# A hand-laid order for all engines in a recommendation kernel on one core: 11 steps a tile, each with a share of every kind of work

## The chip, the cores and the metric

The kernel runs on one core of a Trainium2 chip. A core has a matrix engine (PE, TensorE), a vector engine (DVE), a scalar engine (ACT), GpSimd (POOL), a sequencer for transfers (SP) and 16 DMA engines. Each engine works through its own instruction stream in the order in which the instructions stand there, and waits at an instruction until what it needs is there.

The metric is the time of one execution on the device in microseconds (us). For the kernel before it is 10250.98 us, the median of 3 runs (10248.7 to 10254.62). About 0.2% of that, 20 us, is what a measurement tells from no change.

## What is computed

16384 users, for each 32 token indices, three lists of 20 indices and four single indices. Rows of the word table (50000 x 300) are averaged over the 32 tokens; rows of three small tables (1000, 5000 and 10000 rows of 64) are averaged over the 20 indices; four tables (100, 50, 20 and 1000 rows of 64) give one row each. Each small table has a second, one column wide, whose rows are summed. The features, 748 wide, go through four layers.

```python
tok = word_emb[token_idx].mean(axis=1)
e1 = emb_mh1[mh1_idx].mean(axis=1)
...
o1 = emb_oh1[oh1_idx]
...
emb = jnp.concatenate([tok, e1, e2, e3, o1, o2, o3, o4], axis=1)
wide = (wide_mh1[mh1_idx].sum(axis=(1, 2)) + ... + wide_oh4[oh4_idx][:, 0])[:, None]
h = jax.nn.relu(emb @ W1 + b1)      # 748 -> 1024
h = jax.nn.relu(h @ W2 + b2)        # 1024 -> 512
h = jax.nn.relu(h @ W3 + b3)        # 512 -> 256
return jax.nn.sigmoid(h @ Wd + bd + wide)
```

## The kernel before

The 16384 users are 32 blocks of 512, and a block is four **tiles** of 128 users (one user to a partition).

**Small tables by matmul.** At the start the seven small tables are loaded and laid out in SBUF as 138 slices of 128 rows, each value split into three bf16 terms (`terms`, lines 132 to 155). A lookup with its sum is then a matmul: for each user a matrix of counts, 128 rows by 138 slices, says how often a table row is named. That matrix is made on the chip. `lookup_keys` (lines 200 to 231) turns the indices of a block into row and slice numbers. For eight pairs of users at a time DVE makes one-hot rows (`row1`) and one-hot slices (`slice1`) with a compare (L244), eight pieces a tile in two buffers. PE multiplies them (L255), two matmuls of half the partitions for each pair, 128 a tile, into a PSUM tile `pc` that holds three pairs and has two buffers. ACT writes each `pc` into `cnt` as fp8 (L263), 22 evictions a tile. `small_sums` then runs over the 138 slices, one matmul each with its weights in `cnt` and its data in `terms` (L281), into `pg`, two tables at a time, and DVE adds the three terms of each (L286), four reductions a tile.

**Word table by gathers.** `tokens` (lines 178 to 198) works in eight groups of four tokens. For each group POOL issues four indirect DMAs (L184), each of which fetches one row of 300 floats for each of 128 users, into `tok_rows`, which has three buffers. DVE folds the four to two (L192) and to one (L197) and adds that to `g` (L198); the first group writes `g` itself (L195).

**Layers.** `mlp` runs once a block: PE transposes the features in fp32 (L336), DVE scales them into `x` (L337), then come the layers (L321), 176 products of 128 x 128 by 128 x 512 in fp32, each of which PE runs as several passes, with ACT's relu behind each group of products (L328). Two PSUM buffers `ph` are shared by the transposes, the layers and the output row (L346, L348, sigmoid L352).

**What sets the order.** The program is written tile after tile: one-hots, counts, sums, tokens, wide sums of a tile, and the layers after four tiles. Before, a scheduler sorts each engine's instructions by their place in the program and by what is ready in its model, and so lets the counts of one tile and the sums of another stand between each other. POOL's gathers stay in program order. SP loads the indices.

Of the kernel before, what the change touches and what calls it, by code (L numbers as in the profile page):

```python
# [8 lines left out]
F32 = mybir.dt.float32  # L9
# [17 lines left out]
ONEHOT = 8  # L27
# [14 lines left out]
def kernel(  # L42
# [42 lines left out]
    gp = ctx.enter_context(tc.tile_pool(name="g", bufs=NSUB))  # L85
# [92 lines left out]
    def tokens(g, it):  # L178

        for q in range(N_TOK // TOK_GROUP):  # L180
            rows = tokp.tile([P, TOK_GROUP * TOK_D], F32, name="tok_rows")
            for t in range(TOK_GROUP):
                j = q * TOK_GROUP + t
                nc.gpsimd.indirect_dma_start(  # L184
                    out=rows[:, t * TOK_D : (t + 1) * TOK_D],
                    out_offset=None,
                    in_=word,
                    in_offset=bass.IndirectOffsetOnAxis(ap=it[:, j : j + 1], axis=0),
                )
            n = TOK_GROUP * TOK_D // 2  # L190
            while n > TOK_D:
                nc.vector.tensor_add(rows[:, 0:n], rows[:, 0:n], rows[:, n : 2 * n])  # L192
                n //= 2
            if q == 0:
                nc.vector.tensor_add(g[:, 0:n], rows[:, 0:n], rows[:, n : 2 * n])  # L195
            else:
                nc.vector.tensor_add(rows[:, 0:n], rows[:, 0:n], rows[:, n : 2 * n])  # L197
                nc.vector.tensor_add(g[:, 0:n], g[:, 0:n], rows[:, 0:n])  # L198

    def lookup_keys(blk):  # L200
# [5 lines left out]
        ix = keyp.tile([P, pairs, 2, N_SMALL], I32, name="ix")  # L206
        for s in range(NSUB):
            b0 = blk * BLOCK + s * P
            nc.sync.dma_start(
                out=ix[(s % 2) * HALF : (s % 2 + 1) * HALF, s // 2],  # L210
                in_=idx[b0 : b0 + P, IDX_MH:IDX_COLS].rearrange("(f p) c -> p f c", p=HALF),
            )
        part = keyp.tile([P, 2, pairs, 2, N_SMALL], I32, name="part")
        nc.vector.tensor_single_scalar(part[:, 0], ix, P - 1, op=ALU.bitwise_and)
        nc.vector.tensor_single_scalar(part[:, 1], ix, 7, op=ALU.logical_shift_right)
        keys = keyp.tile([P, pairs, 2, 2 * N_SMALL], BF16, name="keys")
        for r in range(pairs):
            view = keys[:, r].rearrange("p w (f c) -> p w f c", f=2)
            nc.vector.tensor_copy(view[:, 0], part[:, 0, r])
            nc.vector.tensor_add(view[:, 1], part[:, 1, r], first)  # L220
# [12 lines left out]
    def counts(sc, s):  # L233

        cnt = cp.tile([P, 2, HALF, n_h], FP8, name="cnt", tag="counts")
        pc = None
        for b in range(HALF):
            if b % ONEHOT == 0:
                row1 = ohp.tile([P, ONEHOT, P], BF16, name="row1")
                slice1 = ohp.tile([P, ONEHOT, n_h], BF16, name="slice1")  # L240
                hot = (row1, slice1)
                for w, (one, n) in enumerate(((row1, P), (slice1, n_h))):
                    shape = [P, ONEHOT, n // 2, 2]
                    nc.vector.tensor_tensor(  # L244
                        one.rearrange("p i (n d) -> p i n d", d=2),
                        iota[:, 0:n].rearrange("p (n d) -> p n d", d=2).unsqueeze(1).to_broadcast(shape),
                        sc[:, s // 2, w, s % 2, b : b + ONEHOT, :].unsqueeze(2).to_broadcast(shape),
                        ALU.is_equal,
                    )
            k = b % PER_BANK  # L250
            if k == 0:
                pc = ps_c.tile([P, 2, 512], F32, name="pc")
            for f in range(2):
                rows = slice(f * HALF, (f + 1) * HALF)
                nc.tensor.matmul(  # L255
                    pc[:, f, k * n_h : (k + 1) * n_h],
                    hot[0][rows, b % ONEHOT, :],
                    hot[1][rows, b % ONEHOT, :],
                    start=True,
                    stop=True,  # L260
                )
            if k == PER_BANK - 1 or b == HALF - 1:
                nc.scalar.activation(  # L263
                    cnt[:, :, b - k : b + 1, :].rearrange("l f k h -> l f (k h)"),
                    pc[:, :, 0 : (k + 1) * n_h],
                    AF.Copy,
                    scale=0.5,
                    saturate=True,
                )
        return cnt  # L270

    def small_sums(g, cnt):

        by_slice = cnt.rearrange("l f p h -> l (f p) h")
        for i in range(0, len(SMALL), 2):
            pair = SMALL[i : i + 2]
            pg = ps_g.tile([P, 2, 3 * ROW], F32, name="pg")
            for j, f in enumerate(pair):
                h0, h1 = slices[f]
                for h in range(h0, h1):  # L280
                    nc.tensor.matmul(  # L281
                        pg[:, j, :], by_slice[:, :, h], terms[:, h, :], start=(h == h0), stop=(h == h1 - 1)
                    )
            at = TOK_D + i * ROW
# [6 lines left out]
            )  # L291

    def features(it, sc, s):

        g = gp.tile([P, G_COLS], F32, name="g")
        small_sums(g, counts(sc, s))
        tokens(g, it)
# [9 lines left out]
        return g, wide  # L307

    def chunk(g, k):
# [5 lines left out]
        return g[:, at : at + 2 * EMB]  # L315

    def layer(dst, weights, bias, src, kks, n_out):
        for m in range(n_out):
            ph = ps_h.tile([P, BLOCK], F32, name="ph", tag="ph")
            for k, kk in enumerate(kks):  # L320
# [6 lines left out]
                )  # L327
            nc.scalar.activation(dst[:, m, :], ph, AF.Relu, bias=bias[:, m : m + 1])  # L328

    def mlp(blk, gs):  # L330
        x = xp.tile([P, NK, BLOCK], F32, name="x", tag="even")
        for k in range(NK):
            kk = chunk_k[k]
            pt = ps_h.tile([P, BLOCK], F32, name="pt", tag="ph")
            for s, (g, _) in enumerate(gs):
                nc.tensor.transpose(pt[:kk, s * P : (s + 1) * P], chunk(g, k), ident)  # L336
            nc.vector.tensor_scalar(x[:kk, k, :], pt[:kk, :], scale[:kk, k : k + 1], None, ALU.mult)  # L337
        h1 = xp.tile([P, M1, BLOCK], F32, name="h1", tag="odd")
        layer(h1, w1_sb, b1_sb, x, chunk_k, M1)
        h2 = xp.tile([P, M2, BLOCK], F32, name="h2", tag="even")  # L340
        layer(h2, w2_sb, b2_sb, h1, [P] * M1, M2)
        h3 = xp.tile([P, M3, BLOCK], F32, name="h3", tag="odd")
        layer(h3, w3_sb, b3_sb, h2, [P] * M2, M3)
# [3 lines left out]
        for s, (_, wide) in enumerate(gs):  # L347
            nc.tensor.matmul(  # L348
                po[:, s * P : (s + 1) * P], wide, ident, start=False, stop=(s == NSUB - 1)
            )  # L350
# [4 lines left out]
        )  # L355

    for blk in range(B // BLOCK):
        it = idxp.tile([P, NSUB, N_TOK], I32, name="it")
        nc.sync.dma_start(
            out=it,  # L360
            in_=idx[blk * BLOCK : (blk + 1) * BLOCK, 0:N_TOK].rearrange("(s p) c -> p s c", p=P),
        )
        sc = lookup_keys(blk)
        mlp(blk, [features(it[:, s, :].bitcast(U32), sc, s) for s in range(NSUB)])


# [39 lines left out]
```

## Time and profile before

| | us |
|---|---|
| median of 3 runs | 10250.98 |
| the profiled execution's own time | 10252.28 |
| its span, first to last instruction | 10250.5 |
| length of one block (a 32nd of the steady part) | 317.5 |

The profile is one execution. Its page gives each engine's busy time and its share of the span, a strip of 40 equal slices, the DMA queues, the chain of work that ended last, and groups of instructions: line, engine, operation, what it writes and reads, the tile's shape, how often, then busy microseconds and the mean of one in nanoseconds, then the idle time just before them and what ended most of it. PE's weight loads are listed as PEld; they overlap its matmuls. "issue" stands for idle time for which the profile shows no cause. The mean clock granted to PE over the span was 0.709 of full speed. In the busy strip all slices but the first and the last few look alike, so a stretch of a few tiles from the middle can stand for the whole:

```profile
PE   3666666666566656666566665666656666666666
...
DVE  4333333333333343333333333333333333333332
ACT  3222222222222222222222222222222222222222
POOL 5334433334333343333433334333343333433332
PEclk7776667776677766777667776677766777667777
```

### The profile page before, as it was taken

What the parts mean: (1) busy time and instruction counts of PE and PEld (TensorE: products, weight loads), DVE (VectorE), ACT (ScalarE), POOL (GpSimd) and SP (SyncE); (2) the same over time, 40 slices, a digit from 0 to 9 for tenths busy, and PEclk for the clock granted to TensorE, in tenths of its full rate; (3) what the DMA queues carried; (4) which work ended last, traced back from release to release, by engine and by line L of the source; (5) the groups of instructions that cost most, each with busy time, mean ns of one, the idle gap of its engine ahead of it and who ended that gap; (6) DMA issues with size and microseconds to landing.
All of it is one profiled execution on the core that took longest, in us unless ns stands there. A gap on an engine that the chain in (4) does not pass through costs nothing.

```text
span 10250.5 us, 99707 instructions
## 1 busy us (share of the span) xinstructions
PE 6613.1 (65%) x40960; PEld 4044.7 (39%) x40960; DVE 3434.1 (34%) x6209; ACT 2584.4 (25%) x3385; POOL 4006.1 (39%) x4103
## 2 busy tenths in 40 slices
PE   3666666666566656666566665666656666666666
PEld 2443434444344433434334433434334344343444
DVE  4333333333333343333333333333333333333332
ACT  3222222222222222222222222222222222222222
POOL 5334433334333343333433334333343333433332
PEclk7776667776677766777667776677766777667777
DMA  4222222222222222222222222222222222222221
GB/s 118 60 58 68 68 65 58 60 63 72 61 59 59 63 76 60 59 57 63 78 60 59 59 59 78 59 59 59 58 78 59 62 59 59 74 62 62 59 58 44
DMA packets 242805, 652.31 MB, mean 64 GB/s; under 512 B 105631, under 2 KB 109471, under 8 KB 242347
## 3 DMA queue, kind: packets, MB, share of 16 engines
q0 software_dynamic: 196608, 629.41, 22.8%
q1 hardware_dynamic: 42738, 10.83, 0.5%
q8 instruction: 320, 5.24, 0.2%
q10 hardware_dynamic: 3001, 5.69, 0.2%
q14 instruction: 138, 1.13, 0.0%
HBM read 645.59 MB, written 0.07 MB: 63 GB/s over the span
## 4 chain that ended last, share of the span: by engine, by line
issue 59%; POOL 31%; PE 5%; DMA 1%; ACT 1%; DVE 1%; another core or an unknown queue 1%; POOLq 0%; SPq 0%; DVEq 0%; ACTq 0%
POOL tok_rows L184 31%; PE pg L281 2%; PE ph L321 2%; DMA tok_rows<-in_word_emb_dram,it 1%; ACT cnt L263 1%; PE pc L255 0%; DVE slice L244 0%; DMA raw<-in_mh_dram 0%; DVE tok_rows L192 0%; DVE row L244 0%; ACT h L328 0%; PE pt L336 0%; DVE g L286 0%; POOLq L184 0%
## 5 line engine op out<-in xcount | busy, mean ns | idle before, releaser
L184 POOL DMA_INDIRECT tok_rows<-in_word_emb_dram,it x4096 | 4005.2, 978 | 6120.9 <-DVE g L195 3741.5
L281 PE MATMUL pg<-terms,cnt 128*128 128x195 bf16 x17664 | 2323.1, 285 | 2037.1 <-issue 2000.2
L263 ACT ACTIVATE cnt<-pc 128x828 fp8e3<-128x828 f32 (+1 forms) x2816 | 2140.4, 850 | 4317.8 <-PE pc L255 4277.9
L281 PEld LDWEIGHTS <-cnt 128*128 128x128 fp8e3 x17664 | 1927.2, 147 | 2487.5 <-issue 2446.0
L255 PE MATMUL pc<-slice,row 64*128 64x138 bf16 x16384 | 1473.7, 304 | 1004.4 <-ACT cnt L263 695.4
L192 DVE TENSOR_TENSOR tok_rows<-tok_rows 128x600 f32<-128x600 f32 x1024 | 799.7, 781 | 2858.7 <-DMA tok_rows<-in_word_emb_dram,it 2845.8
L321 PE MATMUL ph<-x,w_sb 128*128 128x512 f32 (+1 forms) x3072 | 1462.2, 638 | 449.3 <-ACT h L328 435.2
L255 PEld LDWEIGHTS <-row 64*128 64x128 bf16 x16384 | 869.2, 123 | 1510.0 <-issue 1334.3
L328 ACT ACTIVATE h<-ph,b_sb 128x512 f32<-128x512 f32 x448 | 305.8, 687 | 3292.3 <-PE ph L321 2228.3
L321 PEld LDWEIGHTS ph<-x,w_sb 128*128 128x128 f32 (+1 forms) x3072 | 622.5, 205 | 1270.0 <-issue 771.7
L321 PE MATMUL ph<-h,w_sb 128*128 128x512 f32 x2560 | 1103.9, 592 | 0.0
L286 DVE TENSOR_REDUCE g<-pg 128x130 f32<-128x390 f32 (+1 forms) x512 | 247.8, 510 | 1960.7 <-PE pg L281 1949.5
L244 DVE TENSOR_TENSOR row<-iota,sc 128x1024 bf16<-128x1024 bf16 x1024 | 705.2, 689 | 197.4 <-PE pc L255 178.2
L244 DVE TENSOR_TENSOR slice<-iota,sc 128x1104 bf16<-128x1104 bf16 x1024 | 743.6, 726 | 0.0
L321 PEld LDWEIGHTS ph<-h,w_sb 128*128 128x128 f32 x2560 | 486.4, 190 | 612.3 <-issue 612.3
L227 DVE COPY sc<-pk 128x1024 bf16<-128x1024 bf16 x32 | 39.2, 1225 | 1643.4 <-PE pk L224 1643.4
L198 DVE TENSOR_TENSOR g<-g,tok_rows 128x300 f32<-128x300 f32 x896 | 420.2, 469 | 23.9
L197 DVE TENSOR_TENSOR tok_rows<-tok_rows 128x300 f32<-128x300 f32 x896 | 420.8, 473 | 17.5
L336 PE MATMUL pt<-ident,g 128*128 128x128 f32 (+1 forms) x768 | 221.1, 370 | 102.1 <-DVE sc L227 40.9
L336 PEld LDWEIGHTS pt<-ident,g 128*128 128x128 f32 (+1 forms) x768 | 108.1, 167 | 198.4 <-issue 94.9
L337 DVE TENSOR_SCALAR x<-pt,scale 128x512 f32<-128x512 f32 (+1 forms) x192 | 140.1, 746 | 3.4 <-PE pt L336 0.6
L346 PE MATMUL po<-h,wd_sb 128*1 128x512 f32 x128 | 60.1, 591 | 0.0
(35 smaller groups left out, 391.0 us busy)
## 6 DMA issues: line engine op xcount, KB each, us to landing
tok_rows<-in_word_emb_dram,it POOLq DMA_INDIRECT x4096
ix<-in_idx_dram SPq DMA_DIRECT2D x128, 32.0 KB
w_sb<-in_W_dram ACTq DMA_DIRECT2D x6, 512.0 KB
w_sb<-in_W_dram ACTq DMA_DIRECT2D x1, 2048.0 KB
it<-in_idx_dram SPq DMA_DIRECT2D x32, 64.0 KB
out_dram<-y SPq DMA_DIRECT2D x32, 2.0 KB
raw<-in_mh_dram SPq DMA_DIRECT2D x1, 422.5 KB
w_sb<-in_W_dram ACTq DMA_DIRECT2D x1, 256.0 KB
```

Source lines behind the costliest of these rows:

```text
L184: nc.gpsimd.indirect_dma_start(out=rows[:, t * TOK_D : (t + 1) * TOK_D], out_offset=None, in_=word, in_offset=bass.IndirectOffsetOnAxis(ap ...
L192: nc.vector.tensor_add(rows[:, 0:n], rows[:, 0:n], rows[:, n : 2 * n])
L197: nc.vector.tensor_add(rows[:, 0:n], rows[:, 0:n], rows[:, n : 2 * n])
L198: nc.vector.tensor_add(g[:, 0:n], g[:, 0:n], rows[:, 0:n])
L244: nc.vector.tensor_tensor(one.rearrange("p i (n d) -> p i n d", d=2), iota[:, 0:n].rearrange("p (n d) -> p n d", d=2).unsqueeze(1).to_broa ...
L255: nc.tensor.matmul(pc[:, f, k * n_h : (k + 1) * n_h], hot[0][rows, b % ONEHOT, :], hot[1][rows, b % ONEHOT, :], start=True, stop=True,)
L263: nc.scalar.activation(cnt[:, :, b - k : b + 1, :].rearrange("l f k h -> l f (k h)"), pc[:, :, 0 : (k + 1) * n_h], AF.Copy, scale=0.5, sat ...
L281: nc.tensor.matmul(pg[:, j, :], by_slice[:, :, h], terms[:, h, :], start=(h == h0), stop=(h == h1 - 1))
L286: nc.vector.tensor_reduce(g[:, at : at + n * ROW].rearrange("p (f d) -> p f d", f=n), pg[:, 0:n, :].rearrange("p f (c d) -> p f d c", c=3) ...
L321: nc.tensor.matmul(ph, weights[:kk, k, m * P : (m + 1) * P], src[:kk, k, :], start=(k == 0), stop=(k == len(kks) - 1),)
L328: nc.scalar.activation(dst[:, m, :], ph, AF.Relu, bias=bias[:, m : m + 1])
L336: nc.tensor.transpose(pt[:kk, s * P : (s + 1) * P], chunk(g, k), ident)
```

## The change

The scheduler is switched off (`manual_schedule`), and the program itself writes every engine's order. A tile now has 11 steps. The pieces of work are generators, and a small class, `Paced`, lets each advance by its share at every step. A step holds:

- the counts of six pairs of users of this tile, 12 matmuls and two evictions (the last step four pairs), and the one-hots for the step after it;
- an eleventh of the token groups of this tile: in eight of the eleven steps one group, its gathers and its adds;
- an eleventh of the sums of the **preceding** tile, 13 to 15 matmuls; after the fourth table's pair the count of work takes in a lull of 12;
- a 44th of the layers of the **preceding block**.

At the end of a tile come the wide sums of the preceding one; at the end of a block its six groups of transposes and the copies to `x`, not spread over steps. After the last tile one more round does the last sums, and then the last block's layers run alone. `g` has five buffers instead of four; `tok_rows` keeps three, `onehot` and `counts` two. The index loads of a block are issued in the second tile of the block before it. The order of the tables within the sums is (0, 2, 6, 4) instead of (0, 2, 4, 6). The number of operations of each other kind stays, but the one-hots come in 11 pieces a tile instead of eight.

```diff
-ONEHOT = 8
+ONEHOT = 6
+STEPS = -(-HALF // ONEHOT)
+LULL = 12
...
-    gp = ctx.enter_context(tc.tile_pool(name="g", bufs=NSUB))
+    gp = ctx.enter_context(tc.tile_pool(name="g", bufs=NSUB + 1))
...
     def small_sums(g, cnt):
-        for i in range(0, len(SMALL), 2):
+        for i in (0, 2, 6, 4):
...
+                    if h < h1 - 1:
+                        yield 1
...
+            yield n if i != 6 else n + LULL
...
+    class Paced:
+        def __init__(self, gen, size, n):
+            self.gen, self.size, self.n = gen, size, n
+            self.done = self.part = 0
+        def go(self):
+            self.part += 1
+            while self.done * self.n < self.size * self.part:
+                work = next(self.gen, None)
+                if work is None:
+                    return
+                self.done += work
...
+    mlp_size = NK * M1 + M1 * M2 + M2 * M3 + M3
+    ctx.enter_context(tc.manual_schedule())
...
+    for t in range(tiles + 1):
+        s = t % NSUB
+        sums = None
+        if before:
+            sums = Paced(small_sums(*before), n_h + LULL, STEPS)
+        if t < tiles:
...
+            toks = Paced(tokens(g, it[:, s, :].bitcast(U32)), N_TOK // TOK_GROUP, STEPS)
+        for i in range(STEPS):
+            if t < tiles:
+                hot_now = hot
...
+                if i < STEPS - 1:
+                    hot = one_hots(sc, s, i + 1)
...
+                counts(cnt, hot_now, i)
+                toks.go()
+            if sums:
+                sums.go()
+            if layers:
+                layers.go()
+        if before:
+            sums.finish()
+            gs.append(before[0])
+            wides.append(wide_term(before[0]))
+        before = (g, cnt) if t < tiles else None
+        if len(gs) == NSUB:
+            if layers:
+                layers.finish()
+            layers = Paced(mlp(t // NSUB - 1, transposed(gs), wides), mlp_size, NSUB * STEPS)
+            gs, wides = [], []
+    layers.finish()
```

The lines have new numbers: gathers L184 are now L186, the adds L192, L197 and L198 are L194, L199 and L200, the one-hots L244 are L255, counts L255 are L273, evictions L263 are L280, sums L281 are L298, their reductions L286 are L305, layers L321 are L348 and relus L328 are L357.

The instructions of DVE in the middle of a tile, before. `x2` after a row means two in a row; `tok_rows` are the gathered word rows, `g` the features, `pg` the sums of the small tables.

```order
L286 TENSOR_REDUCE g<-pg 128x130
L195 TENSOR_TENSOR g<-tok_rows 128x300
L198 TENSOR_TENSOR g<-g,tok_rows 128x300 x2
L192 TENSOR_TENSOR tok_rows<-tok_rows 128x600
L197 TENSOR_TENSOR tok_rows<-tok_rows 128x300
L198 TENSOR_TENSOR g<-g,tok_rows 128x300
```

The first add into `g` (L195) stands behind the reduction of the first sums (L286), and the adds of the other groups follow it one after another with nothing between them. The same engine after the change, from a like place:

```order
L255 TENSOR_TENSOR row_6163<-iota,sc 128x768
L255 TENSOR_TENSOR slice_6164<-iota,sc 128x828
L194 TENSOR_TENSOR tok_rows<-tok_rows 128x600
L199 TENSOR_TENSOR tok_rows<-tok_rows 128x300
L200 TENSOR_TENSOR g<-g,tok_rows 128x300
L305 TENSOR_REDUCE g<-pg 128x130
L255 TENSOR_TENSOR row_6208<-iota,sc 128x768
L255 TENSOR_TENSOR slice_6209<-iota,sc 128x828
```

Each group's adds now stand between the one-hots of two steps, with a reduction among them now and then.

ACT before, over one block: the evictions of the counts of four tiles (`cnt` from `pc`), and the relus of the layers (`h` from `ph`) together at its end.

```order
L263 ACTIVATE cnt<-pc 128x2x414 x21
L263 ACTIVATE cnt<-pc 128x2x138
L328 ACTIVATE h_7513<-ph,b_sb 128x512 x8
L328 ACTIVATE h_7578<-ph,b_sb 128x512 x4
L328 ACTIVATE h_7619<-ph,b_sb 128x512 x2
L352 ACT_TABLE_LOAD
L352 ACTIVATE y<-po,bd_sb 1x512
```

And after the change:

```order
L357 ACTIVATE h_30037<-ph,b_sb 128x512
L280 ACTIVATE cnt<-pc 128x2x414 x8
L357 ACTIVATE h_30037<-ph,b_sb 128x512
L280 ACTIVATE cnt<-pc 128x2x414 x3
L280 ACTIVATE cnt<-pc 128x2x138
L280 ACTIVATE cnt<-pc 128x2x414 x4
L357 ACTIVATE h_30037<-ph,b_sb 128x512
```

The relus no longer stand together: a few evictions lie between any two of them.

More of the change, by code (lines that the diff above doesn't have):

```diff
@@ L231, in lookup_keys @@
         return sc
[L233 to L248, printed above, removed]
-                    )
[L250 to L270, printed above, removed]
@@ L306, in features @@
         nc.vector.tensor_add(wide, wide, g[:, G_COLS - 1 : G_COLS])
-        return g, wide
+        return wide
     def chunk(g, k):
@@ L355, in mlp, with finish @@
         )
[L357 to L364, printed above, removed]
+        yield M3
+    class Paced:
[9 more added lines that the diff above has]
+                self.done += work
+        def finish(self):
+            for _ in self.gen:
+                pass
```

114 lines of the change are left out of this document (88 added, 26 removed).

## The prediction, made before the changed kernel ran

> **What bounds the kernel now.** I read the page first: no engine is busy for two thirds of the span, and the chain that ended last is mostly "issue".
>
> ```profile
> span 10250.5 us, 99707 instructions
> PE 6613.1 (65%) x40960; PEld 4044.7 (39%) x40960; DVE 3434.1 (34%) x6209; ACT 2584.4 (25%) x3385; POOL 4006.1 (39%) x4103
> issue 59%; POOL 31%; PE 5%; DMA 1%; ACT 1%; DVE 1%; another core or an unknown queue 1%; POOLq 0%; SPq 0%; DVEq 0%; ACTq 0%
> ...
> L184 POOL DMA_INDIRECT tok_rows<-in_word_emb_dram,it x4096 | 4005.2, 978 | 6120.9 <-DVE g L195 3741.5
> L281 PE MATMUL pg<-terms,cnt 128*128 128x195 bf16 x17664 | 2323.1, 285 | 2037.1 <-issue 2000.2
> L263 ACT ACTIVATE cnt<-pc 128x828 fp8e3<-128x828 f32 (+1 forms) x2816 | 2140.4, 850 | 4317.8 <-PE pc L255 4277.9
> L255 PE MATMUL pc<-slice,row 64*128 64x138 bf16 x16384 | 1473.7, 304 | 1004.4 <-ACT cnt L263 695.4
> ```
>
> The sums (L281) stood idle 2037 us, 2000 of them for nothing that the profile shows. The timeline of one tile shows how that looks:
>
> ```profile
> 5028.10 0.32 PE L281 MATMUL pg<-terms,cnt 128*128 128x195 bf16 x1 [1.08 <-issue]
> 5030.23 0.32 PE L281 MATMUL pg<-terms,cnt 128*128 128x195 bf16 x1 [1.81 <-issue]
> ...
> 5037.22 0.95 POOL L184 DMA_INDIRECT tok_rows<-in_word_emb_dram,it  x1 [0.30 <-issue]
> 5038.48 0.95 POOL L184 DMA_INDIRECT tok_rows<-in_word_emb_dram,it  x1 [0.30 <-issue]
> ...
> 5043.56 1.30 PE L281 MATMUL pg<-terms,cnt 128*128 128x195 bf16 x7 [0.38 <-issue]
> ...
> 5065.64 14.21 PE L281 MATMUL pg<-terms,cnt 128*128 128x195 bf16 x137 [0.75 <-ACT cnt L263]
> ```
>
> With no gather running, 137 sums take 14.21 us. While gathers are issued every 1.26 us (5037.22 to 5038.48), sums come one at a time, some 2 us apart, until 5.1 us after the last gather began. Then they are dense at once. So I asked for the busy time of stretches cut at the gathers (columns: length, then busy us and instructions of PE, PEld, DVE, ACT, POOL; PE clock; DMA):
>
> ```profile
> 4886.89:4917.00 30.11, 11.62 (x98) 9.07 (x96) 6.74 (x12) 0.00 (x0) 22.86 (x24) 0.71 0.44 118
> 4928.81:4941.00 12.19, 7.78 (x80) 4.46 (x80) 8.12 (x14) 9.79 (x13) 8.75 (x8) 0.50 0.38 101
> ...
> 5084.62:5126.40 41.78, 32.33 (x70) 13.61 (x68) 11.47 (x20) 2.75 (x4) 30.73 (x32) 0.92 0.44 118
> ...
> 4941.00:4948.32 7.32, 4.84 (x38) 4.43 (x38) 4.84 (x9) 1.55 (x3) 0.00 (x1) 0.57 0.01 2
> ```
>
> A run of 24 gathers lets PE through 98 matmuls in 30 us, one of 32 lets through 70 in 42 us, but one of 8 beside the counts lets through 80 in 12 us. A burst passes something like a hundred matmuls and then almost none. ACT is caught too: in the run of 32 it did four instructions.
>
> **The bound per tile.** Two prices, each for one of the 128 tiles. Gathers: 32 at 1.26 us, 40.3 us. PE's own work, from its dense rows:
>
> ```profile
> 5143.17 34.50 PE L321 MATMUL ph<-h,w_sb 128*128 128x512 f32 x80
> 5177.60 1.88 PE L346 MATMUL po<-h,wd_sb 128*1 128x512 f32 x4
> 5179.31 1.04 PE L348 MATMUL po<-ident,wide 128*1 128x128 f32 x8
> ...
> 5183.37 0.87 PE L255 MATMUL pc<-slice,row 64*128 64x138 bf16 x12 [0.94 <-DVE slice L244]
> ...
> 5081.89 1.29 PE L336 MATMUL pt<-ident,g 128*128 128x128 f32 x8 [1.20 <-DVE wide L306]
> ```
>
> Sums: 138 at 14.21/137 = 0.104, 14.3 us. Layers: 34.50/80 = 0.43 each, 44 a tile (5632 over 128), 19.0 us. Counts: pairs run side by side; less the last one's 0.30, 0.57 us for five pairs, so 64 pairs take 7.3 us. Transposes and output row: 6 at 0.16 and a quarter of 2.9 us, 1.7 us. Together 42.3 us.
>
> 40.3 + 42.3 = 82.6, and the kernel takes 10250.5/128 = 80.1 us a tile: it runs as if gathers and PE took turns. The order explains why. The gathers wait for DVE's first add (L195), which stands behind the first sum's reduction (L286), so they start when PE is at its densest.
>
> ```profile
> POOL tok_rows L184 <- DVE g L195: 3741.5, 126, 84.0
> ```
>
> **The change part by part.** No work goes away: as many gathers, matmuls, evictions (22 a tile: ten steps of two, then two). What changes is where they stand. Each step has 12 count matmuls, 13 to 15 sums, two fp32 products (four PE matmuls), eight elevenths of a token group. POOL's gathers, in the same order, start when DVE frees one of three buffers; DVE now does that once in 1.4 steps all through the tile. The long runs of 24 and 32 become bursts of four, 5.0 us each.
>
> Costs that I put at nothing. One-hots in 11 pieces instead of 8:
>
> ```profile
> L192 DVE TENSOR_TENSOR tok_rows<-tok_rows 128x600 f32<-128x600 f32 x1024 | 799.7, 781 | 2858.7 <-DMA tok_rows<-in_word_emb_dram,it 2845.8
> ...
> L244 DVE TENSOR_TENSOR row<-iota,sc 128x1024 bf16<-128x1024 bf16 x1024 | 705.2, 689 | 197.4 <-PE pc L255 178.2
> L244 DVE TENSOR_TENSOR slice<-iota,sc 128x1104 bf16<-128x1104 bf16 x1024 | 743.6, 726 | 0.0
> ...
> L197 DVE TENSOR_TENSOR tok_rows<-tok_rows 128x300 f32<-128x300 f32 x896 | 420.8, 473 | 17.5
> ```
>
> From 781 ns for 600 columns and 473 for 300, an instruction has some 165 ns that don't scale; six more a tile are 1.0 us. DVE has 3434/128 = 26.8 us a tile, so 27.8 under a tile of 44 or more: hidden by PE, and without that cover 1.0 us. ACT's 2584/128 = 20.2 us hide likewise; the two evictions of a step (1.7 us) lie beside its sums and layers (1.4 and 1.7 us), where now PE waited 695 us for them. New head-of-line risk: behind a token add that waits for a gather stand the next one-hots, and behind them the counts. One-hots are made a step ahead and three gather groups are in flight, so I cost this at nothing; its price is in a rival.
>
> The sum for a tile:
> - Gathers, never shorter: 40.3 us. Beside DVE's one-hots one was slower, 8.75/8 = 1.09 us in the stretch of 8 against 0.95; for all 32 that is 4.5 us a tile at most. PE passes its work beside that time too, so what it adds here it takes from the third term, and I add nothing.
> - After each burst PE stays slow for a while. It was 5.1 − 1.26 = 3.8 us after 24. If that scales, a burst of four has 0.6 and eight of them 5.1 us; if it is fixed, 30 us; if the stall needs a long burst, nothing. I take 5.1, because a burst of 8 left none that I can see.
> - PE's work that the gathers don't cover. In the stretch of 8 gathers PE was busy 7.78 us; a quarter tile has 8 gathers and 42.3/4 = 10.6 us of work, so 2.8 us are left, four times: 11.2 us. Bounds: 0 when all is covered, 4 x 7.3 = 29 us when every 8 gathers need the shortest recovery seen (the 7.3 us stretch).
> - At a block's end six transpose groups and six DVE copies take turns, some 7 us, 1.7 us a tile.
>
> That is 58.3 us; ends 44 (PE and the block's end alone) and 78 (four times 12.2 + 7.3). The nearest row, 8 gathers with 80 matmuls in 12.2 us, says 49 without any recovery, so I stay in the middle.
>
> Whole run: 128 x 58.3 = 7462, plus the start, plus the end: last sums 14, transposes 7, and a block's layers with nothing beside them, 176 x 0.43 + 3 = 79. The start ends when DVE's last table piece is done at 63 us.
>
> ```profile
> 61.47 1.71 DVE L155 TENSOR_TENSOR raw<-raw,terms 128x1495 f32<-128x1495 f32 x1
> ```
>
> 7462 + 63 + 100 = 7625 us, against a span of 10250.5, a time of 10252.28 for that execution and a median of 10250.98, which are the same to 0.02%.
>
> [...]
>
> **Rivals.**
> 1. *Everything hides.* Bursts of four never bring on the stall, since all three stalls seen came after 5 us or more of gathers. PE at 42.3 + 1.7 bounds: 128 x 44 + 163 = 5800 us. For it: 80 matmuls passed beside 8 gathers. Against it: those followed a rest of 7 us or more, and there will be none. Chance 0.22.
> 2. *ACT is what starves.* It waited 16.56 us in the run of 32, and PE then waited 7.71 for it:
>
> ```profile
> 5116.37 0.69 ACT L328 ACTIVATE h<-ph,b_sb 128x512 f32<-128x512 f32 x1 [16.56 <-issue]
> 5117.11 7.54 PE L321 MATMUL ph<-x,w_sb 128*128 128x512 f32 x12 [7.71 <-ACT h L328]
> ```
>
> Counts have two banks, so a late eviction stops the next step's counts, and PE's order keeps everything behind them. A group then takes its burst, 5.6 with the lag, and 1.4 steps of evictions after it, 2.3 us, with 1 us of PE: 8.9, so 71 us and 9250. Against it: beside 8 gathers ACT did 13. Chance 0.2.
> 3. *Slower: PE's clock stays at half.* The stretch of 8 gathers had PE busy 7.78 of 12.19 us and a granted clock of 0.50. If the mixed steps never raise it, layers cost twice 19.0, sums 0.155 each (the row of 7 in 1.30) or 21.4, counts 7.3, the rest 3.4: 70 us, and with 11 uncovered 81 to 83, 10,700 us. It is slower from 78.8 us a tile on, (10250.5 − 163)/128. Against it: dense fp32 products stand in every step, and beside them the clock was 0.92. Chance 0.08. [...]
> 4. *Turns again.* The order spreads the gathers, but PE and gathers still exclude each other: 77 to 79 us, 10,050 to 10,250. Chance 0.07; a fifth of it within 0.2%.
>
> The instructions do move as said, so that the change does nothing is no case.
>
> **Numbers.** The forecast, 50 to 66 us a tile, has 0.43. The range leaves out the best fifth of rival 1's side and rivals 3 and 4: 5750 to 9500 us. About 0.2% (20 us) is what a measurement here can tell from no change. Faster 0.90, same 0.02, slower 0.08.
>
> **What would show it.** Right: POOL's gathers in groups of four all through the span; the stretch between two such groups 6 to 8 us; idle "issue" of the sums below 500 us; PE's clock above 0.8; hardly any "DVE g" wait on POOL over 20 us. Rival 1 shows POOL idle under 10%; rival 2 PE's counts waiting for ACT by 1000 us and more; rival 3 a clock near 0.5; rival 4 sums at 2 us spacing still. A wrong step would be the recovery after a burst, which no row shows for four gathers.

## The result and the profile after

The changed kernel takes 7659.19 us, the median of 4 runs (7632.91 to 7665.39), the kernel before 10252.8 us beside it (10248.7 to 10279.32). The ratio is 0.7461, with a 95% interval of 0.7439 to 0.7483. The prediction was 7625 us, in a range of 5750 to 9500. The profiled execution is the one of 7632.91 us.

From the page of the changed kernel: the span, the engines, the chain that ended last, and four groups.

```profile
span 7631.1 us, 100300 instructions
PE 5876.7 (77%) x40960; PEld 3502.6 (46%) x40960; DVE 3534.9 (46%) x6977; ACT 2659.7 (35%) x3383; POOL 4052.0 (53%) x4103
...
PE 51%; another core or an unknown queue 23%; ACT 10%; issue 9%; DVE 4%; POOL 3%; DMA 0%; DVEq 0%; SPq 0%; ACTq 0%; POOLq 0%
...
L186 POOL DMA_INDIRECT tok_rows<-in_word_emb_dram,it x4096 | 4051.1, 989 | 3442.7 <-DVE g L200 1363.5
L280 ACT ACTIVATE cnt<-pc 128x828 fp8e3<-128x828 f32 (+1 forms) x2816 | 2235.8, 840 | 3547.7 <-remote 1763.9
L298 PE MATMUL pg<-terms,cnt 128*128 128x195 bf16 x17664 | 2166.4, 274 | 350.9 <-issue 255.2
...
L273 PE MATMUL pc<-slice,row 64*128 64x138 bf16 x16384 | 874.2, 233 | 1219.9 <-ACT cnt L280 909.0
```

The sums' unexplained idle time fell from 2000 to 255 us, and the chain is PE's for half of the span instead of "issue" for 59%. The gathers take as long as before (989 ns instead of 978). But the word "remote" is new: ACT waited 1764 us for something that the profile cannot name. A stretch of the timeline shows what that is. First PE, then ACT and DVE:

```profile
4012.95 0.42 PE L298 MATMUL pg<-terms,cnt 128*128 128x195 bf16 x3 [0.80 <-issue]
4014.41 0.49 PE L298 MATMUL pg<-terms,cnt 128*128 128x195 bf16 x3 [1.04 <-issue]
4014.70 3.57 PE L348 MATMUL ph<-h,w_sb 128*128 128x512 f32 x4
4020.35 0.36 PE L273 MATMUL pc<-slice,row 64*128 64x138 bf16 x6 [2.08 <-ACT cnt L280]
...
4017.28 0.69 ACT L357 ACTIVATE h<-ph,b_sb 128x512 f32<-128x512 f32 x1 [6.29 <-remote]
...
4020.19 0.56 DVE L255 TENSOR_TENSOR row<-iota,sc 128x768 bf16<-128x768 bf16 x1 [6.79 <-remote]
```

This is the stall of before in another place: four matmuls of the layers that take 1.91 us at 4005.35 take 3.57, the sums come in threes, ACT stands for 6.29 and DVE for 6.79 us. (The program has 88 products of the layers in a block, and the trace shows 5632 matmuls for them, 176 a block: two for each product.) POOL had begun a run of gathers at 4002.95 and issued its twelfth at 4017.41. The same run cut in three, up to 9 us, to its end, and the pause behind it (length; PE, PEld, DVE, ACT, POOL busy and instructions; clock; DMA):

```profile
4002.95:4012.00 9.05, 9.05 (x80) 5.97 (x79) 4.53 (x9) 3.34 (x4) 6.92 (x8) 0.92 0.37 103
4012.00:4020.30 8.30, 4.43 (x12) 1.88 (x11) 1.44 (x4) 1.55 (x3) 4.98 (x5) 0.79 0.40 111
4020.30:4024.53 4.23, 3.79 (x27) 3.07 (x27) 3.64 (x7) 2.26 (x3) 0.00 (x1) 0.63 0.02 4
```

For nine microseconds PE passes 80 matmuls beside eight gathers, as if they were not there. In the next eight it passes 12. This run is no exception here: the 174 runs of twelve pass 69.6 matmuls on average in their first 9 us, where plain_loads (below) passes 72, and then 15.4 in the 6.5 us that are left. Counting all gathers of the trace, with a pause of 2.2 us between two starts as the end of a run, there are 410 runs: 41 of four gathers, 161 of eight, 174 of twelve, 32 of sixteen, two longer. So the gathers are **not** in bursts of four. POOL fills all buffers that are free, DVE frees more while the run goes on, and when DVE itself stands POOL runs out of buffers and the run ends: 456 of POOL's waits end with an add of DVE's into `g` (L200 and L197, below). After the stretch above DVE and PE go on 2.8 and 2.9 us after the last gather's start. Over the trace DVE stands for over 3 us at the last gather of 304 of the 410 runs and goes on 2.7 us (median) after its start, ACT at 224 of them and 2.5 us.

POOL's longest waits, each with what ended it (us in all, times, longest us; "issue" is the 0.3 us between the gathers of a run):

```profile
POOL tok_rows L186 <- DVE g L200: 1363.5, 338, 8.0
POOL tok_rows L186 <- issue: 1099.4, 3566, 1.6
POOL tok_rows L186 <- DVE g L197: 911.1, 118, 16.2
```

Two questions are left. Is it the stalling that the change cut, or something in the order itself? And what does the stall go by?

### The profile page after: what moved, and what is told of

Read it like the earlier page. It is cut to its first block, busy times and chain, and to the rows that moved or that the text cites. A ratio compares the mean times of both kernels' runs of the same rounds, so it can differ in the third digit from the quotient of the medians.

```text
span 7631.1 us, 100300 instructions
## 1 busy us (share of the span) xinstructions
PE 5876.7 (77%) x40960; PEld 3502.6 (46%) x40960; DVE 3534.9 (46%) x6977; ACT 2659.7 (35%) x3383; POOL 4052.0 (53%) x4103
## 3 DMA queue, kind: packets, MB, share of 16 engines
q0 software_dynamic: 196608, 629.41, 30.0%
## 4 chain that ended last, share of the span: by engine, by line
PE 51%; another core or an unknown queue 23%; ACT 10%; issue 9%; DVE 4%; POOL 3%; DMA 0%; DVEq 0%; SPq 0%; ACTq 0%; POOLq 0%
PE ph L348 22%; PE pg L298 18%; PE pc L273 9%; ACT cnt L280 8%; POOL tok_rows L186 3%; ACT h L357 2%; PE pt L340 1%; DVE x L341 1%; DVE g L305 1%; PE po L370 1%; DVE slice L255 0%; DVE tok_rows L194 0%; PE po L372 0%; DVE tok_rows L199 0%
## 5 line engine op out<-in xcount | busy, mean ns | idle before, releaser
L186 POOL DMA_INDIRECT tok_rows<-in_word_emb_dram,it x4096 | 4051.1, 989 | 3442.7 <-DVE g L200 1363.5
L280 ACT ACTIVATE cnt<-pc 128x828 fp8e3<-128x828 f32 (+1 forms) x2816 | 2235.8, 840 | 3547.7 <-remote 1763.9
L298 PE MATMUL pg<-terms,cnt 128*128 128x195 bf16 x17664 | 2166.4, 274 | 350.9 <-issue 255.2
L255 DVE TENSOR_TENSOR row<-iota,sc 128x768 bf16<-128x768 bf16 (+1 forms) x1408 | 763.5, 542 | 2947.3 <-remote 1625.3
L298 PEld LDWEIGHTS <-cnt 128*128 128x128 fp8e3 x17664 | 1783.4, 147 | 602.7 <-issue 463.6
L273 PE MATMUL pc<-slice,row 64*128 64x138 bf16 x16384 | 874.2, 233 | 1219.9 <-ACT cnt L280 909.0
L273 PEld LDWEIGHTS <-row 64*128 64x128 bf16 x16384 | 566.3, 98 | 2343.3 <-issue 1831.2
L348 PE MATMUL ph<-x,w_sb 128*128 128x512 f32 (+1 forms) x3072 | 1605.6, 650 | 20.4 <-issue 19.9
L348 PE MATMUL ph<-h,w_sb 128*128 128x512 f32 x2560 | 1366.8, 660 | 21.4 <-issue 20.4
L348 PEld LDWEIGHTS ph<-x,w_sb 128*128 128x128 f32 (+1 forms) x3072 | 588.4, 211 | 489.6 <-issue 480.4
L255 DVE TENSOR_TENSOR slice<-iota,sc 128x828 bf16<-128x828 bf16 (+1 forms) x1408 | 805.0, 572 | 0.0
L194 DVE TENSOR_TENSOR tok_rows<-tok_rows 128x600 f32<-128x600 f32 x1024 | 793.7, 775 | 4.9 <-DMA tok_rows<-in_word_emb_dram,it 4.9
L357 ACT ACTIVATE h<-ph,b_sb 128x512 f32<-128x512 f32 x448 | 308.2, 688 | 1220.0 <-remote 507.5
L348 PEld LDWEIGHTS ph<-h,w_sb 128*128 128x128 f32 x2560 | 494.6, 214 | 410.1 <-issue 409.7
L305 DVE TENSOR_REDUCE g<-pg 128x130 f32<-128x390 f32 (+1 forms) x512 | 250.9, 508 | 836.5 <-remote 396.0
L199 DVE TENSOR_TENSOR tok_rows<-tok_rows 128x300 f32<-128x300 f32 x896 | 423.7, 473 | 30.8
L200 DVE TENSOR_TENSOR g<-g,tok_rows 128x300 f32<-128x300 f32 x896 | 421.8, 471 | 30.7
L340 PE MATMUL pt<-ident,g 128*128 128x128 f32 (+1 forms) x768 | 126.6, 299 | 59.7 <-DVE x L341 59.7
```

The lines of the kernel that those rows point to most:

```text
L186: nc.gpsimd.indirect_dma_start(out=rows[:, t * TOK_D : (t + 1) * TOK_D], out_offset=None, in_=word, in_offset=bass.IndirectOffsetOnAxis(ap ...
L255: nc.vector.tensor_tensor(one[:, 0:rows, :].rearrange("p i (n d) -> p i n d", d=2), iota[:, 0:n].rearrange("p (n d) -> p n d", d=2).unsque ...
L273: nc.tensor.matmul(pc[:, f, k * n_h : (k + 1) * n_h], hot[0][half, k0 + k, :], hot[1][half, k0 + k, :], start=True, stop=True,)
L280: nc.scalar.activation(cnt[:, :, b + k0 : b + k0 + n, :].rearrange("l f k h -> l f (k h)"), pc[:, :, 0 : n * n_h], AF.Copy, scale=0.5, sat ...
L298: nc.tensor.matmul(pg[:, j, :], by_slice[:, :, h], terms[:, h, :], start=(h == h0), stop=(h == h1 - 1))
L305: nc.vector.tensor_reduce(g[:, at : at + n * ROW].rearrange("p (f d) -> p f d", f=n), pg[:, 0:n, :].rearrange("p f (c d) -> p f d c", c=3) ...
```

## The experiments

Theory **S**: runs of gathers longer than some 9 us stop the other engines, and the change gains by having fewer such stalls. Rival **O**: the order itself, its chain of one-hots, counts, evictions and two count banks, sets the time, before and after. All twelve kernels were timed once, beside a run of the kernel before on the same chip (10211.6 to 10250.24 us). The four runs of the changed kernel lie within 0.4%, so differences of some per cent count, smaller ones don't. Kernels with plain loads or fewer gathers leave token indices out: they are experiments and no candidates.

### The orders without POOL's gathers

**plain_loads**: the changed kernel, the same bytes by plain loads.

```diff
-                nc.gpsimd.indirect_dma_start(
-                    out=rows[:, t * TOK_D : (t + 1) * TOK_D],
-                    out_offset=None,
-                    in_=word,
-                    in_offset=bass.IndirectOffsetOnAxis(ap=it[:, j : j + 1], axis=0),
-                )
+                nc.sync.dma_start(
+                    out=rows[:, t * TOK_D : (t + 1) * TOK_D],
+                    in_=word[j * P : (j + 1) * P, :],
+                )
```

> Each gather is replaced by a plain load of the same 128 x 1200 bytes from SP's queue (fixed rows of the word table, so the token indices are left out). Theory S with POOL's gathers as the cause: no stall, 5700 to 6300 us. Rival B (the transferred bytes beside the compute are the cause, whoever issues them): PE, ACT and DVE still stop, 7200 us or more. Rival O: 7200 to 7600 us.

Measured: 5234.46 us, below all windows, since PE needs less than the prediction had (see "PE as the floor"). **before_plain** is the same edit in the kernel before.

> The kernel before with each gather replaced by a plain load of the same bytes from SP (fixed rows, token indices left out): what the order before costs with no gathers of POOL's. Theory S (the change gained by less stalling beside gathers): 5600 to 6300 us, so that before 10250 less this is some 4200 us of stall, against 7633 - 5234 = 2400 after. Rival O (the order before was itself bad, and the change gained by mending it): 7500 us or more.

Measured: 7007.91 us, outside both windows, between them. **few_gathers** keeps the changed order and four gathers a tile:

```diff
-            rows = tokp.tile([P, TOK_GROUP * TOK_D], F32, name="tok_rows")
-            for t in range(TOK_GROUP):
+            if q == 0:
+                rows = tokp.tile([P, TOK_GROUP * TOK_D], F32, name="tok_rows")
+            for t in range(TOK_GROUP if q == 0 else 0):
```

> This kernel issues only the first group's four gathers of each tile and adds that one buffer eight times: 28 of 32 gathers are left out, all other work stays. Theory S (a run of gathers that lasts longer than some 9 us stops PE, ACT and DVE until about 3 us after its last one, and this is what the tile's 58 us hold above PE's 44): PE becomes the bound, 128 x 44 + 163 = 5800 us, 5600 to 6100; PE passes its full 320 matmuls a tile at an even rate. Rival O (the order itself costs the time: one-hots, counts, eviction and the reuse of two count banks form a chain of some 5 us a step): 7200 to 7600 us, since that chain is all there.

Measured: 5332.14 us, below S's window for the same reason. The first row below is about a block of plain_loads, the second one of the changed kernel, the third one of the kernel before, in the windows' columns:

```profile
3000.00:3160.00 160.00, 158.49 (x1281) 96.11 (x1280) 109.74 (x218) 80.97 (x106) 0.00 (x0) 1.00 0.45 124
```

```profile
4000.00:4234.00 234.00, 187.74 (x1302) 110.47 (x1301) 111.60 (x223) 82.82 (x106) 127.99 (x128) 0.88 0.31 86
```

```profile
5000.00:5318.00 318.00, 207.31 (x1286) 125.70 (x1286) 106.82 (x193) 80.75 (x107) 126.20 (x129) 0.71 0.24 64
```

Each row holds about a block's 1280 matmuls. Without gathers the new order does them in 160 us, 40 a tile, with PE dense and at a granted clock of 1.00, though 124 GB/s flow beside it. So the bytes are not the cause, and the new order has hardly any slack of its own (PE busy 158.49 of 160 us): O falls for the kernel after. For the kernel before, O is half right. The four times (7633 is the changed kernel's profiled execution, 10250 the kernel before's run beside plain_loads; before_plain ran on a chip where the kernel before took 10211.6, which would make the 843 some 805):

| us | POOL's gathers | plain loads | difference |
|---|---|---|---|
| order before | 10250 | 7008 | 3242 |
| order after | 7633 | 5234 | 2399 |
| difference | 2617 | 1774 | 843 |

Of the 2617 us, 1774 are there with no gather at all; 843 are less stall, if the two simply add. What costs the order before 7008 us stands in the timeline of before_plain, in one tile's counts:

```profile
3550.54 0.53 PE L253 MATMUL pc<-slice,row 64*128 64x138 bf16 x6 [0.22 <-ACT cnt L261]
3551.30 0.53 PE L253 MATMUL pc<-slice,row 64*128 64x138 bf16 x6 [0.23 <-ACT cnt L261]
3552.05 0.53 PE L253 MATMUL pc<-slice,row 64*128 64x138 bf16 x6 [0.22 <-ACT cnt L261]
...
3560.77 13.27 PE L279 MATMUL pg<-terms,cnt 128*128 128x195 bf16 x137
```

Before, a tile's counts stand together, and every six of them wait for ACT's eviction of the bank that they need: one turn is 0.755 us, 22 turns 16.6 us. The whole stretch as a window, with ACT busy nearly throughout (16.22 of 16.80 us) and PE at a granted clock of 0.57:

```profile
3543.90:3560.70 16.80, 10.91 (x133) 6.76 (x132) 12.34 (x24) 16.22 (x22) 0.00 (x0) 0.57 0.04 9
```

In plain_loads, where sums and layers stand between the counts of two steps, the counts hardly wait for anything (41.7 us in all):

```profile
L271 PE MATMUL pc<-slice,row 64*128 64x138 bf16 x16384 | 756.3, 223 | 41.7 <-DVE slice L253 21.5 <-ACT cnt L278 20.1
```

Busy and idle together they take (756.3 + 41.7)/128 = 6.2 us a tile. The difference to 16.6 is 10.4 us a tile, 1330 us in all, three quarters of the 1774. That is read from these rows; a kernel with only the counts spread was not run.

### What the stall goes by

**half_rows**: as many gathers, half the bytes.

```diff
+    HALF_D = TOK_D // 2
+    half_word = word.rearrange("v (h d) -> (v h) d", h=2)
...
-                    out=rows[:, t * TOK_D : (t + 1) * TOK_D],
+                    out=rows[:, t * HALF_D : (t + 1) * HALF_D],
...
-                    in_=word,
+                    in_=half_word,
```

> As many gathers as in the changed kernel, each of 128 x 150 floats instead of 128 x 300 (half of the word table's columns left out; DVE's adds of them are shorter, 10 us a tile instead of 13.5). If the bytes bring the stall on: 6200 to 6800 us. If it goes by gathers and their descriptors: 7300 to 7700 us, as before this cut.

Measured: 7528.1 us, in the second window. That descriptors have a part in it was the author's supposition and was not shown; what the trace counts is gathers and packets. The queue's row in its page (packets, MB, share), and the same row of plain loads issued by POOL, **pool_plain**:

```profile
q0 software_dynamic: 196608, 314.83, 18.6%
```

```profile
q0 software_dynamic: 196608, 629.41, 40.9%
...
L186 POOL DMA_DIRECT2D tok_rows<-in_word_emb_dram x4096 | 2169.7, 537 | 2930.6 <-DVE g L198 1781.2
```

> The changed kernel with plain loads of the same bytes, but issued by POOL (fixed rows, token indices left out). If it is POOL's writing of descriptors, whatever for, that stops the other engines: 7200 to 7900 us, with PE in single matmuls after about 9 us of a run. If only the indirect form does so: 5200 to 5500 us.

Measured: 5240.39 us, in the window of the indirect form. What POOL does within an issue no run shows, only how long it is busy. Half the bytes change the time by 1.4 to 1.7%; the full bytes on the same queue in the same 196608 packets, issued by POOL in the plain form, bring on no stall at all (6 us above plain_loads' 5234.46). But a plain load keeps POOL for 537 ns, a gather for 989: POOL's load fell as well, to 17 us a tile, and mix2 below has gathers of about that load (16 us) with hardly any cost. By the times alone pool_plain does not tell the indirect form from the time that POOL spends.

The traces do tell them apart. An eviction can start when ACT's previous instruction and the last of its bank's matmuls have ended. How long after the later of the two it does start, for all 2816 evictions:

| kernel | over 1 us late | longest, us | in all, us a tile |
|---|---|---|---|
| plain_loads | 0 | 0.38 | 0.4 |
| pool_plain | 0 | 0.38 | 0.4 |
| few_gathers | 81 | 1.99 | 1.5 |
| mix2 | 73 | 5.28 | 1.8 |
| mix3 | 409 | 7.77 | 10.7 |
| changed kernel | 630 | 14.07 | 16.5 |

In few_gathers POOL works 3.8 us a tile and evictions are late; in pool_plain it works 17 and none is. So it is the indirect form, or the scattered rows that come with it, and not POOL's time. The trace of the changed kernel also shows what the word "remote" hides. The matmuls of 629 of the 630 late evictions ended within a run of gathers (ends as the profile models them), and 612 of the 630 start within 0.1 us after a recorded update of the semaphore of PE that they wait for. ACT is not slow there, an eviction takes 840 ns against 850 before. **What is late is the update from PE**, the signal that the trace records: in those 612 it stands 4.5 us (median) behind the end of the bank's last matmul, and in 605 of them PE had by then begun further matmuls, 18 in the median. Whether PE gives the signal late or it is held on its way, the trace does not tell. The trace also has only 11791 of the engines' 13976 updates, so the profile often cannot name who released whom; in plain_loads it names PE for 1772.3 of the 1774.2 us that the evictions waited, and "remote" for none of its longest waits.

**mix2** and **mix3** vary the number of gathers at the same bytes: two or three tokens of each group by gathers, the others by SP's plain loads.

```diff
+                if t < 2:
                     nc.gpsimd.indirect_dma_start(
...
+                else:
+                    nc.sync.dma_start(
```

> Two of the four tokens of each group by gathers, the other two by plain loads of the same bytes from SP (fixed rows, so half of the token indices are left out): 16 gathers a tile. If every gather has its price (2400 us of stall over 4096 gathers, 0.59 us each): 5233 + 2048 x 0.59 = 6430 us, 6200 to 6700. If only runs of some 9 us and more stop the engines: 16 gathers are 20 us of a tile of 41, the runs stay short, 5230 to 5500 us.

Measured: 5298.31 us, in the window of runs.

> Three of four tokens by gathers, one by plain loads (a quarter of the token indices left out): 24 gathers a tile. By a price for every gather: 5233 + 3072 x 0.59 = 7030 us, 6800 to 7200. By runs: they still leave 10 us of pause in a tile of 41, 5300 to 6300 us. A bend between 16, 24 and 32 gathers would speak for runs or for how densely they stand.

Measured: 6460.22 us, outside both windows. With 16 gathers a tile hardly anything stalls; from 16 to 24 each further gather costs (6460 - 5298)/1024 = 1.13 us, from 24 to 32 it costs (7633 - 6460)/1024 = 1.15 us. That is a bend and then two nearly equal steps, and the slope is close to the 1.25 us (median) from one gather to the next. A constant price for every gather falls. What stays the same is the time outside the gathers: with 24, 49.2 us a tile less 30.0 us of gathers leave 19.2; with 32, 58.3 less 40.2 leave 18.1. (A tile is the span less 165 us for start and end, over 128.) The work is not split that way, though: of the changed kernel's 40960 matmuls 30530 start within runs (up to 1.25 us after the last gather's start), which is 75% in 71% of the time. The pauses are hardly denser than the runs: the stall reaches some 3 us beyond the last gather's start, 2.8 to 2.9 us in the stretch above. The runs in mix2 hold two to six gathers (one has eight), and a window of it shows PE as dense as without any (158.19 us busy of 160, in plain_loads 158.49):

```profile
3000.00:3160.00 160.00, 158.19 (x1272) 95.40 (x1271) 109.08 (x217) 80.17 (x105) 64.33 (x64) 1.00 0.45 125
```

### Shorter runs, finer pieces, wider spacing

**bufs2**: two token buffers instead of three.

```diff
-    tokp = ctx.enter_context(tc.tile_pool(name="tok", bufs=3))
+    tokp = ctx.enter_context(tc.tile_pool(name="tok", bufs=2))
```

> Two token buffers instead of three, so no run of gathers is longer than eight (10 us) unless a buffer comes free within it. Theory S: runs end about when the stall would begin; 6500 to 7200 us. Rival O: less work in flight, 7600 to 8300 us.

Measured: 7868.07 us, in O's window and not in S's. Its runs did not get short: 199 of its 443 runs have twelve gathers where its two buffers hold eight, so DVE freed a buffer while the run went on. So it gave up lead and did not do what it was meant to test.

**group2_b3** and **group2_b6**: groups of two tokens (`TOK_GROUP = 2`), with three and with six buffers.

> Token groups of two instead of four with three buffers: at most six gathers in flight, 7.6 us; DVE's adds are 16 x 0.94 = 15.0 us a tile instead of 13.5. Theory S: hardly any stall, 6100 to 6900 us. Rival O: 7600 us or more. If POOL waits for its buffers too often, both are hidden by gathers: then POOL's idle time before its gathers grows over the 3443 us of the changed kernel.

Measured: 7334.42 us, between the two windows.

> Groups of two with six buffers: the same adds as with three, but up to 12 gathers in flight instead of six. If the length of a run of gathers sets the stall: slower than the 7334 us of three buffers, 7500 to 7900. If three buffers gained by something else (adds in smaller pieces): 7200 to 7400 us.

Measured: 7215.1 us, in the second window. More gathers in flight were not slower, against what S said. The number of runs rose to 512 and 505, from 410, and the two kernels have nearly the same number.

**group1_b12**: one gather, one add, twelve buffers.

```diff
-TOK_GROUP = 4
+TOK_GROUP = 1
...
+            if q == 1:
+                nc.vector.tensor_add(g[:, 0:TOK_D], last, rows)
+            elif q > 1:
+                nc.vector.tensor_add(g[:, 0:TOK_D], g[:, 0:TOK_D], rows)
+            last = rows
```

> Groups of one token with twelve buffers: a gather, then one add of 300 columns (32 x 0.47 = 15.0 us of DVE a tile, as for groups of two). If smaller pieces were what brought 7633 down to 7215 with groups of two: 6800 to 7150 us. If it was the lead of the buffers or the shorter runs: 7150 to 7400 us.

Measured: 7157.61 us, at the edge of two windows; 491 runs. It is the fastest kernel with all gathers, 6.5% under 7659, from one run.

**pause128**: a fill by POOL behind each gather.

```diff
+                nc.gpsimd.memset(idle[:, 0:128], 0.0)
```

> A fill of 128 x 128 floats by POOL behind each gather, so that gathers start some 1.6 us apart instead of 1.26; all work stays. If their density stops the engines: POOL's 32 x 1.6 = 51 us bound a tile, 6500 to 7200 us. If every gather has its price whatever its distance: 7600 to 8300 us.

Measured: 7237.33 us, between the windows. The fill was shorter than assumed:

```profile
L194 POOL MEMSET idle<- 128x128 f32 x4096 | 904.6, 221 | 2.1
```

The gathers' starts moved from 1.25 to 1.34 us only, so the run does not decide on density. It does show that POOL can be given 0.22 us more for each gather and the kernel gains, though nothing else changed.

Put together, S needs mending in three places.

**How often runs end does not set the time.** Groups of two and of one have more runs (512, 505, 491 against 410) and are faster; but bufs2 has more too, 443, and is slower, and pause128 has fewer, 364, and is faster. The number of runs does not order these kernels.

**A long run does not stop PE as such.** The kernel before has 32 runs of 32 gathers, 40 us each, beside the layers. In the one that the prediction shows, from 5084.62, PE goes on at 0.43 us a matmul for 25 us:

```profile
5083.36 26.04 PE L321 MATMUL ph<-x,w_sb 128*128 128x512 f32 x60 [0.18 <-DVE x L337]
```

It stands then, for 7.71 us, where it needs a buffer that ACT has yet to empty. The first three relus begin 0.04 us after the product that they need, the fourth 12.1 us after it (5104.25 to 5116.37). In before_plain no relu begins later than 0.04 us. So the 9 us are what stretches with counts and sums show (69.6 matmuls, then 15.4 in the runs of twelve), and beside the layers alone 60 matmuls went on for 26.04 us.

**What the trace shows to be late is, in good part, PE's updates.** Late evictions add up to 16.5 us a tile in the changed kernel, of the 18 that it takes longer than plain_loads. They overlap other waits, so this sum is no price. It is not the whole either: beside gathers the sums (L281 before) also come one at a time where the trace shows no wait, 2.13 us from one to the next at 5028.10 and 2000.2 us of such idle time in all. Whether the onset goes by time, by the number of instructions passed or by the number of signals was not tested.

## Why the prediction came out

**The sum and its terms.** Predicted 58.3 us a tile and 163 us around it; measured (7631.1 - 165)/128 = 58.3, with 44.4 us before the first count and 121.1 after the last (7510.0 to 7631.1). Gathers: 40.3 predicted, (4051.1 + 1099.4)/128 = 40.2 from the rows above. The rest: 5.1 + 11.2 + 1.7 = 18.0 predicted, and POOL's other idle time is (3442.7 - 1099.4)/128 = 18.3.

**Recovery after bursts of four: the split failed.** The step was "a burst of four has 0.6 and eight of them 5.1 us", with bursts of four because DVE would free a buffer "once in 1.4 steps all through the tile". DVE does so only while it does not stand itself, as it does for over 3 us at the end of 304 of the 410 runs; the runs have ten gathers on average. There is no small recovery behind each of 1024 bursts but a stall within most of 410 runs. That 18.0 met 18.3 is luck. The 5.1 us priced bursts of which there are few (41 runs have four gathers). The 11.2 us took 7.78 us of busy PE, in a row with 80 matmuls, nearly all counts, at a clock of 0.50, for 7.78 us of work; by the prediction's own price for counts (7.3 us for 128) they are 4.6, which would have left 6.0 us of each 10.6 and 24 us a tile. What was right is that bursts and their lag, and not PE, set the tile.

**"A burst passes something like a hundred matmuls and then almost none": misread for the run of 32.** Its 70 matmuls in 42 us are layers at 0.43 us, 30 us of work (PE was busy for 32.33): it is the run beside which PE did best, and the row of its fourth relu, 16.56 us of waiting, already held the late start, 12.1 us after the product.

**Gathers and PE taking turns, 82.6 against 80.1: right sum, wrong parts.** That reading priced PE's counts at 7.3 us from its densest row and took the gathers' stall for the rest. The counts were paced by ACT at 16.6 us a tile. The prediction saw both rows (695 us of PE waiting for ACT, a clock of 0.50 in that stretch) and put the edit that spreads the evictions under "costs that I put at nothing"; it should have stood there as a gain. Some 68% of the gain, 1774 of 2617 us, is the order's own.

**PE as the floor, 42.3 + 1.7,** was mis-sized: plain_loads needs 160 us a block, 40 a tile, at a clock of 0.999 over the span. The counts fit into 6.2 us instead of 7.3; a sum follows the other after 0.087 us there (median), not 0.104.

**The small terms.** Six more one-hot instructions a tile: 1.0 us predicted, (3534.9 - 3434.1)/128 = 0.8 measured, hidden. Gathers beside one-hots: up to 4.5 us a tile feared, 989 ns against 978 measured, 0.4 us.

**The rivals.** Everything hides, 5800 us: it does so with 16 gathers a tile (mix2, 5298 us), and its objection (no rest between the bursts) was the right one. ACT starves, with PE waiting for it 1000 us and more: the row has 909, and the chain is the one forecast, a late eviction that stops the counts and all that stands behind them. But 612 of the 630 late evictions start with a late update of PE's, within the stall and not after each burst, and the 71 us a tile were too much. Half clock: 0.874 over the span; fallen. Turns again, at 77 us and more: fallen, since 75% of the matmuls start within runs.

**The bytes and the stall.** plain_loads and pool_plain show PE dense beside the bytes: 124 and 125 GB/s, a clock of 1.00, and 158.49 and 158.40 us busy of 160. The run of twelve gathers shows it dense only at first: busy in all of the first 9.05 us, with 80 matmuls, and in 4.43 of the next 8.30, with 12. What was seen late there are updates of PE's semaphore; DVE's adds of 600 columns take as long as without gathers (775 ns, in plain_loads 776).

**What stays open.** Why PE's updates are late beside indirect gathers, and why PE's sums also slow down with no wait to be seen, was not found. Bytes and the number of packets do not explain it (pool_plain has the same 629.41 MB in 196608 packets and no late eviction), nor does POOL's time (17 us a tile there, 3.8 in few_gathers with 81 late). The plain loads also fetch 128 rows that lie together, always the same, where the gathers fetch scattered ones; that was not separated from the indirect form. All times on record come with a recorded span; whether the stall is there without recording, no run shows.

## What to carry to other kernels

Give a suspected wait a kernel without its cause, in both orders, before splitting a gain: here the two together told an order that paced PE by ACT (0.755 us a turn) from a stall that looked like the whole story. When a wait is put down to nothing, measure it from the end of what the instruction needs to its start, beside a kernel without the suspect: that told 630 late starts, up to 14.07 us, from a slow engine (840 ns an eviction, as before). Spread an operation that is paced by another engine (counts and their evictions, 16.6 us a tile together, 6.2 spread in plain_loads) between work that is not, rather than only overlapping its total. And spreading its consumers need not spread a transfer that is issued as fast as buffers come free (here 410 runs of ten gathers on average, where the program has groups of four): look at the run lengths in the trace, not at the program's order.

## What was not expected of the hardware

- Beside indirect gathers updates of PE's semaphore came late: in the changed kernel 630 of 2816 evictions began over 1 us after all that they needed had ended, up to 14.07 us, 612 of them within 0.1 us after such an update; beside plain loads (plain_loads, pool_plain) none was later than 0.38 us.
- 16 gathers a tile of 40 us cost 1.2% (mix2, 5298 against 5234 us in plain_loads), four 1.9% (few_gathers, 5332); from 16 to 24 and to 32 each further one costs 1.13 and 1.15 us, nearly its full spacing of 1.25.
- The same 629 MB in the same 196608 packets issued by POOL as plain loads cost 0.1% (5240 against 5234 us), at 537 ns an instruction instead of 989.
- Halving a gather's bytes does not shorten it much on POOL, 980 ns in half_rows against 989:

```profile
L189 POOL DMA_INDIRECT tok_rows<-in_word_emb_dram,it x4096 | 4012.2, 980 | 3377.5 <-DVE g L205 1305.2
```
